# A two-layer graph network on one core: the set-up's score sums move into the feature matmul, its staging into the main pass's buffers, its stores to SyncE's queue

## The chip, the cores and the metric

The kernel runs on 1 core of one Trainium2 chip. A core has five engines, each with its own in-order instruction stream: TensorE (PE, with its weight loads listed as PEld), VectorE (DVE), ScalarE (ACT), GpSimd (POOL) and SyncE (SP). Data moves between the chip's memory (HBM) and the on-chip memory (SBUF) by DMA transfers, which SyncE, ScalarE and GpSimd issue; TensorE writes its results to a separate small memory, PSUM, of eight banks. The metric is device time in microseconds (us). The kernel before takes 2074.67 us, the median of 3 runs (2074.32 to 2076.41).

## The reference

`x` has 4096 rows of 512; `adj` is a 4096 x 4096 matrix of zeros and ones, symmetric with a full diagonal. Layer 0 is a graph attention with 8 heads of 64 features:

```python
feats = jnp.einsum('nf,hfo->hno', X, W)
s_self = jnp.einsum('hno,ho->hn', feats, a_self)
s_neigh = jnp.einsum('hno,ho->hn', feats, a_neigh)
dense = s_self[:, :, None] + s_neigh[:, None, :]
dense = jnp.where(dense > 0, dense, ALPHA * dense)
dense = dense * A[None, :, :]
attn = jax.nn.softmax(dense, axis=-1)
out = jnp.einsum('hij,hjo->hio', attn, feats) + b[:, None, :]
```

then a relu, a residual and a layer norm. Layer 1 is a dot-product attention within 32 graphs of 128 rows, with a residual and a layer norm. The change lies wholly in the preparation of layer 0: the features, the two scores of each row and head, and exponentials of the scores.

## The kernel before

**Set-up (lines 592 to 813).** `x` is taken in eight blocks `k` of four 128-row tiles `u`. For each block:

- `load_rows` (L608): SyncE loads four 128 x 512 tiles `xt_f`; the pool `xtp` has four buffers, so the next block's loads wait for this block's transposes.
- `turn_rows` (L652, L655): TensorE transposes the block, 16 pieces of 128 x 128, and ScalarE copies the four results from PSUM to `xT_f`.
- `scores` (L663, L671): TensorE multiplies the transposed block by `wa`, the 512 x 16 matrix of weights times score vectors, which VectorE makes once at the start (L638, L641); ScalarE copies the result.
- `exponentials` (L677 to L708): a small matmul with `stack` adds the four partial sums and turns them so that rows lie on partitions; ScalarE takes five exponentials for the block, VectorE splits them into parts (`e_b`, `e_p`, `nb_all`).
- `features` (L734, L742), per tile: four matmuls with 512 columns each (the four 128-row chunks of `W`, all 8 heads), then VectorE adds the bias to give `fb`.
- `scaled_features` (L748, L756, L757, L769), per tile: VectorE multiplies `fb` by an exponential (`gst`), ScalarE and VectorE make a rounded and a rest part (`fst`), and GpSimd's queue stores both to HBM (`g_d` 256 KB, `f_d` 512 KB). `fb`, `gst` and `fst` have three buffers each, in pools of the set-up's own.
- `rows_of_exponentials` and `columns_of_exponentials` (L713, L717, L721, L726, L727): the exponentials of the own score are transposed to rows, stored to `pu_d` from GpSimd's queue, and transposed back in another order.

All of these PSUM results come from one pool, `ps_setup`, of seven buffers. One more bank, `ps_misc`, is for later work. GpSimd's queue also loads the first three blocks of the adjacency with a cast to 8 bits (`load_adjacency`, L587), after blocks 3, 4 and 5.

**Main pass (`main_pass`, L1306 on).** Four passes `r`, one for each pair of heads; in each, four column blocks of 1024 and 32 tiles `j` of 128 rows, taken eight at a time in the first three passes (`wide=8`) and four at a time in the last. For each `j`, VectorE makes a tile `q` for each head from the A^T tile `at` (L1367), ScalarE a mark (L1376), and TensorE accumulates `accf` (L1387), `acc` (L1407) and `dens` (L1421). In the first pass `bring` (L1113, L1117, L1118) transposes the adjacency on TensorE, ScalarE widens it into `at`, and GpSimd's queue stores it; later passes load it back (L1103). `at` and `q` have six buffers each for the whole kernel; the first three passes have six more for `at` and two more for `q`, which `ring` hands out in turn. SyncE's queue loads `f_s`, `g_s` (the stored features, L1348, L1352), `p_row`, `u_row` (broadcast rows of `pu_d`, L1312, L1315), and `ck`, blocks of the adjacency that a check of the inputs reads. After the main pass's last steps come the pieces of layer 1, dealt into the last pass by a written plan.

**What sets the order.** TensorE's order is the program's own (`manual_schedule`); that of the other engines, and of the loads and stores on their queues, is decided when the program is built, by a scheduler that places each instruction where it expects it to be ready. On each engine, and on each queue's issuing engine, instructions then run in that fixed order. SBUF is laid out in pools; pools with `side="right"` are stacked from the other end.

Of the kernel before, what the change touches and what calls it, by code (L numbers as in the profile page):

```python
# [19 lines left out]
P = 128  # L20
# [384 lines left out]
def adjacency_streamed_path(  # L405
# [50 lines left out]
    const = ctx.enter_context(tc.tile_pool(name="fconst", bufs=1))  # L456
    first_pass = ExitStack()
# [25 lines left out]
    for c in range(FC):  # L483
# [6 lines left out]

    stack = const.tile([P, 2 * H], F32, name="stack")
    nc.vector.tensor_reduce(
        stack,
        ident.rearrange("p (c k) -> p k c", c=FC)[:, : 2 * H, :],
        AX.X,
        OP.add,
    )
# [56 lines left out]
    more = {}  # L554

    def ring(name, pool, n):

        if name not in more:
            return pool
        k = turns[name] % (n + more[name][1])  # L560
        turns[name] += 1
        return pool if k < n else more[name][0]

    def partial_sums(dst, wide, rhs):

        for c in range(FC):
            nc.tensor.matmul(
                dst[32 * c : 32 * c + 32, :], wide[:, c, :32], rhs[:, c, :], start=True, stop=True
            )
# [22 lines left out]
    with tc.tile_pool(name="setup1", bufs=1, side="right") as one, tc.tile_pool(  # L592
        name="setup2", bufs=2, side="right"
    ) as two, tc.tile_pool(name="setup3", bufs=3, side="right") as three, tc.tile_pool(
        name="xtp", bufs=4, side="right"
    ) as xtp, tc.tile_pool(name="ps_setup", bufs=7, space=PSUM) as pss:
        NB = NT // 4
        xts, xTs, sts, pu_js, rows = {}, {}, {}, {}, {}
# [13 lines left out]
        w_sb = one.tile([P, FC, H * FH], F32, name="w_sb_f")  # L612
        for c in range(FC):
            nc.scalar.dma_start(
                w_sb[:, c].rearrange("p (h o) -> p h o", h=H),
                W[:, ts(c, P), :].rearrange("h p o -> p h o"),
            )
        a_b2 = three.tile([P, PR, 2, FP], F32R, name="fst").bitcast(F32)
        a_b2 = a_b2.rearrange("p r s n -> p (r s n)").rearrange(
            "p (k h o) -> p k h o", k=2, h=H  # L620
        )
# [11 lines left out]
        wa = one.tile([P, FC, 32], F32, name="wa")  # L633
        nc.vector.memset(wa, 0.0)
        for c in range(FC):
            for k in range(2):
                prod = three.tile([P, H, FH], F32, name="fb")
                nc.vector.tensor_mul(  # L638
                    prod, w_sb[:, c].rearrange("p (h o) -> p h o", h=H), a_b2[:, k]
                )  # L640
                nc.vector.tensor_reduce(wa[:, c, k * H : (k + 1) * H], prod, AX.X, OP.add)  # L641
        xs = one.tile([P, FC, NB], F32, name="xs")

        def turn_rows(k):
# [4 lines left out]
            for u, c in order if k == 0 else sorted(order, key=lambda x: x[1]):  # L649
                if u == 0:  # L650
                    pts[c] = pss.tile([P, 4, P], F32, name="ps_set")
                nc.tensor.transpose(pts[c][:, u, :], xts[k][u][:, ts(c, P)], ident)  # L652
# [6 lines left out]
        def scores(k):  # L659

            ps = pss.tile([P, 4 * P], F32, name="ps_set")
            for c in range(FC):
                nc.tensor.matmul(  # L663
                    ps[32 * c : 32 * c + 32, :],
                    wa[:, c, :],
                    xTs[k][:, c].rearrange("p u n -> p (u n)"),
                    start=True,
                    stop=True,
                )
            st = sts[k] = one.tile([P, 4 * P], F32, name="st")  # L670
            nc.scalar.copy(st, ps)  # L671

        def exponentials(k):
            blk = slice(4 * k, 4 * k + 4)
            pts = pss.tile([P, 4, 2, H], F32, name="ps_set")
            for u in range(4):
                nc.tensor.matmul(  # L677
                    pts[:, u].rearrange("p k h -> p (k h)"),
                    tile_j(sts[k], u),
                    stack,  # L680
                    start=(u == 0),
                    stop=True,
                    skip_group_check=True,
                )
            s_c, t_c = pts[:, :, 0, :], pts[:, :, 1, :]
            nc.scalar.activation(e_all[:, blk, 1, :], t_c, AF.Exp)
            nc.scalar.activation(e_all[:, blk, 0, :], t_c, AF.Exp, scale=ALPHA)
            nc.scalar.activation(d_all[:, blk, :], t_c, AF.Exp, scale=ALPHA - 1.0)
            pu_j = pu_js[k] = two.tile([P, 4, 2, H], F32, name="pu_j")
            nc.scalar.activation(pu_j[:, :, 1, :], s_c, AF.Exp, scale=-ALPHA)  # L690
            nc.scalar.activation(pu_j[:, :, 0, :], s_c, AF.Exp, scale=1.0 - ALPHA)


# [16 lines left out]
        def rows_of_exponentials(k):  # L710
# [5 lines left out]
            row = rows[k] = one.tile([2 * H, 4 * P], F32, name="pu_row")  # L716
# [14 lines left out]
        def features(k, u):  # L731
            pf = pss.tile([P, H * FH], F32, name="ps_set")
            for c in range(FC):
                nc.tensor.matmul(  # L734
                    pf,
                    tile_j(xTs[k][:, c].rearrange("p u n -> p (u n)"), u),
                    w_sb[:, c, :],
                    start=(c == 0),
                    stop=(c == FC - 1),
                )  # L740
            fb = three.tile([P, H, FH], F32, name="fb")
            nc.vector.tensor_add(fb.rearrange("p h o -> p (h o)"), pf, b_row)  # L742
            return fb

        def scaled_features(k, u, fb):
            j = 4 * k + u
            gst = three.tile([P, PR, 2, FH], F32, name="gst")
            nc.vector.tensor_tensor(  # L748
                gst.rearrange("p r h o -> p (r h) o"),
# [4 lines left out]
            fst = three.tile([P, PR, 2, FP], F32R, name="fst")  # L754
# [10 lines left out]
            for dst, n, src in (  # L765
                (g_d, FP, gst.rearrange("p r h o -> p r (h o)")),
                (f_d, 2 * FP, fst.rearrange("p r s n -> p r (s n)").bitcast(F32)),
            ):
                nc.gpsimd.dma_start(dst[:, k, :, ts(u, n)].rearrange("r p n -> p r n"), src)  # L769

        turn_rows(0)
        for k in range(NB):
            if k + 1 < NB:
                load_rows(k + 1)
            fbs = [features(k, 0)]
            if k == 0:
                fbs.append(features(k, 1))
                scores(0)
            else:
                exponentials(k)  # L780
            if k + 1 < NB:
                turn_rows(k + 1)
            if k == 0:
                exponentials(0)
            scaled_features(k, 0, fbs[0])
            if k:
                fbs.append(features(k, 1))
                columns_of_exponentials(k - 1)
            scaled_features(k, 1, fbs[1])
            fbs.append(features(k, 2))  # L790
            scaled_features(k, 2, fbs[2])
            if k + 1 < NB:
                scores(k + 1)
            rows_of_exponentials(k)
            if k == NB - 1:
                xsum = one.tile([P, FC], F32, name="xsum")
                nc.vector.tensor_reduce(xsum, xs, AX.X, OP.add)
                xsum_b = one.tile([P, FC, 32], F32, name="xsum_b")
                nc.vector.tensor_copy(xsum_b, xsum[:, :, None].to_broadcast([P, FC, 32]))
# [729 lines left out]
```

## Time and profile before

| What | Value |
|---|---|
| Median of 3 runs | 2074.67 us (2074.32 to 2076.41) |
| Profiled execution, its own time | 2074.4 us |
| Its span, first to last instruction | 2072.1 us |
| Mean granted TensorE clock | 0.996 of full |
| Busy: TensorE / VectorE / ScalarE / GpSimd | 2040.3 / 1663.9 / 1536.7 / 247.5 us |
| Moved by DMA | 551.28 MB, mean 266 GB/s |
| First feature matmul (L734) / last one ends | 9.8 us / 161.55 us |
| First adjacency transpose (L1113) / first `accf` matmul (L1387) | 162.62 us / 168.37 us |

The page of the profile gives busy time per engine; the chain of waits follows what ended last, back through whatever released it; the windows give busy time, granted clock and DMA share in stretches of time; the groups give the number and mean time of one kind of instruction. "f32 128x512" is 128 partitions by 512 elements. Times of the windows and the chain count from the span's start.

### The profile page before, as it was taken

To read this page: it belongs to the slowest core of one execution; us is meant where nothing else is said; L and a number is where in the kernel's file an instruction comes from. 1 tells how busy PE (TensorE), PEld (TensorE's weight loads), DVE (VectorE), ACT (ScalarE), POOL (GpSimd) and SP (SyncE) were. 2 spreads that over 40 slices of the span, in tenths; PEclk is the share of its full clock that TensorE was granted. 3 is DMA by queue.
4 is the path that set the end of the run, shared out by engine and by line. 5 is a ranking of instruction groups with operands and counts; after the bars stand their busy time and mean duration, and the time that the engine had idled before them with its cause. 6 is when DMAs were issued, how large, how long until landed. Compare 5 with 4: busy or idle time off the path is not lost.

```text
span 2072.1 us, 37981 instructions
## 1 busy us (share of the span) xinstructions
PE 2040.3 (98%) x14934; PEld 999.7 (48%) x14934; DVE 1663.9 (80%) x2058; ACT 1536.7 (74%) x1821; POOL 247.5 (12%) x393
## 2 busy tenths in 40 slices
PE   8999999999999999999999999999999999999997
PEld 4555555444445444444445444544454444545443
DVE  5557888888799998798999999999975984885654
ACT  3338898888878899788889889998885666567420
POOL 2343222222100000000000000000210210210111
PEclk9999999999999999999999999999999999999999
DMA  8999999999899999788999899989974763775211
GB/s 252 265 258 248 272 293 265 296 261 297 264 332 349 361 334 338 261 312 300 315 318 337 312 342 327 325 292 361 325 234 144 245 243 132 227 272 168 71 49 43
DMA packets 207881, 551.28 MB, mean 266 GB/s; under 512 B 25292, under 2 KB 66252, under 8 KB 207692
## 3 DMA queue, kind: packets, MB, share of 16 engines
q1 hardware_dynamic: 140748, 425.79, 59.4%
q0 software_dynamic: 62784, 121.91, 23.4%
q8 instruction: 119, 1.95, 0.4%
q10 hardware_dynamic: 4160, 1.05, 0.2%
q14 instruction: 70, 0.57, 0.1%
HBM read 491.79 MB, written 107.22 MB: 289 GB/s over the span
## 4 chain that ended last, share of the span: by engine, by line
PE 81%; DMA 8%; issue 5%; DVE 3%; ACT 2%; POOL 1%; POOLq 0%; SPq 0%; DVEq 0%; ACTq 0%
PE acc L1407 35%; PE accf L1387 20%; DMA at_d<-at 5%; PE ps_m L1050 5%; PE ps_m L978 5%; PE dens L1421 5%; PE ps_set L734 4%; DVE q L1367 1%; PE ps_m L1005 1%; PE ps_m L1064 1%; ACT mark L1376 1%; DMA xt_f<-in_x_dram 1%; PE ps_m L907 1%; PE ps_m L1113 1%; PE ps_m L958 1%
## 5 line engine op out<-in xcount | busy, mean ns | idle before, releaser
L1367 DVE SCALAR_TENSOR_TENSOR q<-p_row,d_all,at 128x1024 f32<-128x1024 f32 x1024 | 1242.6, 1280 | 159.2 <-PE acc L1407 130.1
L1376 ACT ACTIVATE mark<-q,nb_all 128x1024 fp8e4<-128x1024 f32 x896 | 994.2, 1145 | 173.1 <-DVE q L1367 158.1
L1407 PE MATMUL acc<-q,g_s 128*32 128x512 f32 x8192 | 903.3, 593 | 1.1 <-DVE q L1367 0.4
L1407 PEld LDWEIGHTS acc<-q,g_s 128*32 128x32 f32 x8192 | 264.6, 110 | 594.5 <-issue 533.7
L1387 PE MATMUL accf<-at,f_s 128*128 128x512 f32 x2048 | 493.3, 397 | 1.9 <-issue 1.8
L1387 PEld LDWEIGHTS accf<-at,f_s 128*128 128x128 f32 x2048 | 379.3, 188 | 110.6 <-issue 29.1
L1132 ACT ACTIVATE ck<-ck,neg_half_f 128x1024 f32<-128x1024 f32 x128 | 146.0, 1140 | 22.1 <-DMA ck<-in_adj_dram 22.1
L1133 ACT ACTIVATE ck<-ck,neg_quarter 128x1024 f32<-128x1024 f32 x128 | 146.3, 1143 | 1.9
L1117 ACT CAST at<-ps_m 128x1024 fp32r<-128x1024 fp8e4 x128 | 120.2, 1025 | 8.7 <-PE ps_m L1113 5.6
L1421 PE MATMUL dens<-mark,e_b 128*6 128x512 fp8e4 x2048 | 124.4, 379 | 0.7 <-ACT mark L1376 0.7
L734 PE MATMUL ps_set<-w_sb_f,xT_f 128*128 128x512 f32 x256 | 117.3, 607 | 0.1
L978 PE MATMUL ps_m<-x1T,M_sb 128*128 128x512 f32 x256 | 113.1, 595 | 1.6 <-ACT x1T L959 1.6
L1050 PE MATMUL ps_m<-wvT,x1T 128*128 128x512 f32 x256 | 114.2, 594 | 0.0
L1252 POOL DMA_DIRECT2D hs_d<-hst x12 | 10.7, 894 | 834.0 <-DVE hst L1242 740.0
L1372 DVE TENSOR_SCALAR mark<-q,d_all 128x1024 fp8e4<-128x1024 f32 x128 | 96.0, 750 | 5.1 <-DVE q L1367 0.5
L1421 PEld LDWEIGHTS <-e_b 128*6 128x6 bf16 x2048 | 52.8, 86 | 80.4 <-issue 37.0
L1118 POOL DMA_DIRECT2D at_d<-at x128 | 68.8, 538 | 170.5 <-ACT at L1117 106.9
L756 ACT ACTIVATE fst<-fb 128x512 fp32r<-128x512 f32 x32 | 20.3, 636 | 83.9 <-DVE fb L742 52.9
L978 PEld LDWEIGHTS ps_m<-x1T,M_sb 128*128 128x128 f32 x256 | 47.9, 190 | 63.0 <-issue 59.9
L1050 PEld LDWEIGHTS ps_m<-wvT,x1T 128*128 128x128 f32 x256 | 47.6, 190 | 57.2 <-issue 56.0
L985 ACT ACTIVATE zT<-ps_m,zb 128x512 f32<-128x512 f32 x32 | 21.8, 683 | 71.0 <-PE ps_m L978 71.0
L734 PEld LDWEIGHTS ps_set<-w_sb_f,xT_f 128*128 128x128 f32 x256 | 49.2, 200 | 51.5 <-issue 50.2
(185 smaller groups left out, 1117.9 us busy)
## 6 DMA issues: line engine op xcount, KB each, us to landing
at<-at_d SPq DMA_DIRECT2D x384, 512.0 KB, 6.1
ck<-in_adj_dram SPq DMA_DIRECT2D x128, 512.0 KB, 5.5
f_s<-f_d SPq DMA_DIRECT2D x128, 512.0 KB, 7.3
at_d<-at POOLq DMA_DIRECT2D x128, 512.0 KB, 14.9
g_s<-g_d SPq DMA_DIRECT2D x128, 256.0 KB, 5.7
f_d<-fst POOLq DMA_DIRECT2D x32, 512.0 KB, 8.5
p_row<-pu_d SPq DMA_DIRECT2D x32, 512.0 KB, 6.9
a_b<-in_adj_dram POOLq DMA_DIRECT2D x32, 512.0 KB, 16.4
```

Of the source, the lines that this page charges most:

```text
L734: nc.tensor.matmul(pf, tile_j(xTs[k][:, c].rearrange("p u n -> p (u n)"), u), w_sb[:, c, :], start=(c == 0), stop=(c == FC - 1),)
L978: nc.tensor.matmul(pz, L1["M"][:, f, ts(c, P)], x1T[:, f, :], start=(f == 0), stop=(f == FC - 1),)
L1050: nc.tensor.matmul(pv, x1T[:, f, ts(u, P)], L1["wvT"][:, f, :], start=(f == 0), stop=(f == FC - 1),)
L1117: nc.scalar.copy(at, both[:, :, k])
L1132: tc.keep_in_program_order(nc.scalar.activation(ck, ck, AF.Square, bias=neg_half))
L1133: nc.scalar.activation(ck, ck, AF.Abs, bias=neg_quarter, accum_out=binp[:, k : k + 1])
L1367: nc.vector.scalar_tensor_tensor(q, p_row[h], d_j, ats[r, c, j].bitcast(F32), op0=OP.max, op1=OP.mult)
L1372: nc.vector.tensor_scalar(mark, q, d_j, None, op0=OP.is_gt, saturate=False)
L1376: nc.scalar.activation(mark, q, AF.Sigmoid, bias=nb_all[:, j, hh : hh + 1], scale=BIG, saturate=False,)
L1387: nc.tensor.matmul(accf[:, s, :], f_s[j // 4][:, j % 4, w, :], ats[r, c, j][:, ts(s, HB)], start=(j == 0 and w == 0), stop=(j == NT - 1 an ...
L1407: nc.tensor.matmul(acc[o : o + 32, s, :], g_s[j // 4][:, j % 4, h, o % FH : o % FH + 32], qs[j, h][:, ts(s, HB)], start=(j == 0), stop=(j ...
L1421: nc.tensor.matmul(dens[lo : lo + 6, :], e_b[:, j, 2 * r + h, :], marks[j, h][:, ts(s, HB)], start=(j == 0), stop=(j == NT - 1),)
```

## The change

- **Scores in the feature matmul.** The weight tile `w_sb` gets two more columns for each head (`FW = FH + 2`): the weights times the two score vectors. A feature matmul now gives 8 x 66 columns. Since that is more than one PSUM bank holds, it is issued as two matmuls of four heads (264 columns) each, into two banks; the features have a PSUM pool of their own, `ps_feat`, of two such pairs, and the other set-up results keep three buffers. `scores`, the `stack` matmul and `wa` go. The first three tiles are made without score columns (256 columns a matmul), and `first_scores` adds theirs with 12 small matmuls.
- **Exponentials per tile.** VectorE multiplies a tile's scores by constants (`powers`), two small instructions, and ScalarE takes three exponentials per tile instead of five per block. Their parts are made at the end of the block (`parts_of_exponentials`), and the row and column transposes of a block move into the block after it.
- **Staging.** `fb` and `gst` are the two halves of a tile of the main pass's pool `q`, `fst` is a tile of its pool `at`: six buffers each instead of three. The pool `setup3` goes.
- **Stores.** `g_d` and `f_d` are written from SyncE's queue instead of GpSimd's.
- **A^T buffers apart.** The six further `at` buffers are allocated at the start on the right side, and `ring` hands them out ahead of the first six.

```diff
@@ adjacency_streamed_path
+    wide_passes = ExitStack()
+    at2 = wide_passes.enter_context(tc.tile_pool(name="more_at", bufs=MORE, side="right"))
     first_pass = ExitStack()
...
-    stack = const.tile([P, 2 * H], F32, name="stack")
...
-    more = {}
+    more = {"at": (at2, MORE)}
 
     def ring(name, pool, n):
 
         if name not in more:
             return pool
-        k = turns[name] % (n + more[name][1])
+        pool_2, m = more[name]
+        k = turns[name] % (n + m)
         turns[name] += 1
-        return pool if k < n else more[name][0]
+        if name == "at":
+            return pool_2 if k < m else pool
+        return pool if k < n else pool_2
...
-    ) as two, tc.tile_pool(name="setup3", bufs=3, side="right") as three, tc.tile_pool(
-        name="xtp", bufs=4, side="right"
-    ) as xtp, tc.tile_pool(name="ps_setup", bufs=7, space=PSUM) as pss:
+    ) as two, tc.tile_pool(name="xtp", bufs=4, side="right") as xtp, tc.tile_pool(
+        name="setup_rows", bufs=1, side="right"
+    ) as late, tc.tile_pool(name="ps_setup", bufs=3, space=PSUM) as pss, tc.tile_pool(
+        name="ps_feat", bufs=2, space=PSUM
+    ) as psf:
...
-        w_sb = one.tile([P, FC, H * FH], F32, name="w_sb_f")
+        FW = FH + 2
+        w_sb = one.tile([P, FC, H, FW], F32, name="w_sb_f")
...
-        wa = one.tile([P, FC, 32], F32, name="wa")
-        nc.vector.memset(wa, 0.0)
         for c in range(FC):
+            prod = qp.tile([P, C], F32, name="q").rearrange("p (k h o) -> p k h o", k=2, h=H)
             for k in range(2):
-                prod = three.tile([P, H, FH], F32, name="fb")
...
-                nc.vector.tensor_reduce(wa[:, c, k * H : (k + 1) * H], prod, AX.X, OP.add)
+                nc.vector.tensor_mul(prod[:, k], w_sb[:, c, :, :FH], a_b2[:, k])
+                nc.vector.tensor_reduce(w_sb[:, c, :, FH + k], prod[:, k], AX.X, OP.add)
+        powers = one.tile([P, 5, H], F32, name="powers")
+        for i, v in enumerate((ALPHA, 1.0, ALPHA - 1.0, 1.0 - ALPHA, -ALPHA)):
+            nc.vector.memset(powers[:, i, :], v)
...
-                    pts[c] = pss.tile([P, 4, P], F32, name="ps_set")
+                    last = k == 0 and c == FC - 1
+                    pts[c] = misc([P, 4, P]) if last else pss.tile([P, 4, P], F32, name="ps_set")
...
-        def scores(k):
...
-        def exponentials(k):
+        def exponentials(k, u, sc):
+
+            j = 4 * k + u
+            if u == 0:
+                pu_js[k] = two.tile([P, 4, 2, H], F32, name="pu_j")
+            st = small.tile([P, 5, H], F32, name="st")
+            for lo, hi, w in ((0, 3, 1), (3, 5, 0)):
+                nc.vector.tensor_tensor(
+                    st[:, lo:hi].rearrange("p k (q h) -> p k q h", q=2),
+                    sc[:, None, :, :, w].to_broadcast([P, hi - lo, 2, H // 2]),
+                    powers[:, lo:hi].rearrange("p k (q h) -> p k q h", q=2),
+                    OP.mult,
+                )
+            nc.scalar.activation(e_all[:, j], st[:, 0:2], AF.Exp)
+            nc.scalar.activation(pu_js[k][:, u], st[:, 3:5], AF.Exp)
+            nc.scalar.activation(d_all[:, j, :], st[:, 2], AF.Exp)
+
+        def parts_of_exponentials(k):
...
         def features(k, u):
-            pf = pss.tile([P, H * FH], F32, name="ps_set")
+            pf = psf.tile([P, 2, HB], F32, name="ps_fe")
+            pf = pf[:, :, : H * FW // 2].rearrange("p q (h w) -> p q h w", w=FW)
+            scored = k > 0 or u == 3
+            cols = slice(0, FW if scored else FH)
             for c in range(FC):
...
+                for q in range(2):
+                    nc.tensor.matmul(
+                        pf[:, q, :, cols],
+                        tile_j(xTs[k][:, c].rearrange("p u n -> p (u n)"), u),
+                        w_sb[:, c, 4 * q : 4 * q + 4, cols],
+                        start=(c == 0),
+                        stop=(c == FC - 1),
+                    )
+            both = qp.tile([P, C], F32, name="q").rearrange("p (s h o) -> p s h o", s=2, h=H)
...
+            if scored:
+                exponentials(k, u, pf[:, :, :, FH:])
+            return both
+
+        def first_scores():
+
+            ps = pss.tile([P, 4, H, 2], F32, name="ps_set")
...
+        def scaled_features(k, u, both):
             j = 4 * k + u
-            gst = three.tile([P, PR, 2, FH], F32, name="gst")
+            fb, gst = both[:, 0], both[:, 1]
...
-            fst = three.tile([P, PR, 2, FP], F32R, name="fst")
+            fst = atp.tile([P, C], F32R, name="at").rearrange(
+                "p (r s n) -> p r s n", r=PR, s=2
+            )
...
-                nc.gpsimd.dma_start(dst[:, k, :, ts(u, n)].rearrange("r p n -> p r n"), src)
+                nc.sync.dma_start(dst[:, k, :, ts(u, n)].rearrange("r p n -> p r n"), src)
...
+            fbs = {}
+            for u in range(4):
+                fbs[u] = features(k, u)
+                if u == (0 if k else 2) and k + 1 < NB:
+                    turn_rows(k + 1)
+                if u == 1 and k:
+                    rows_of_exponentials(k - 1)
+                if u == 2 and k:
+                    columns_of_exponentials(k - 1)
+                if u == 2 and k == 0:
+                    first_scores()
+                    for v in range(3):
+                        scaled_features(k, v, fbs[v])
+                if k or u == 3:
+                    scaled_features(k, u, fbs[u])
...
+            parts_of_exponentials(k)
             if k in (3, 4, 5):
                 tc.keep_in_program_order(load_adjacency(0, 4 * (k - 3)))
+        rows_of_exponentials(NB - 1)
...
-    at2 = wide_passes.enter_context(tc.tile_pool(name="more_at", bufs=MORE))
     q2 = wide_passes.enter_context(tc.tile_pool(name="more_q", bufs=2))
-    more["at"], more["q"] = (at2, MORE), (q2, 2)
+    more["q"] = (q2, 2)
```

In the compiled order of the changed kernel, the stores stand on SyncE between the loads of `x` and the first `f_s`, `g_s`, `p_row` and `u_row` loads, and GpSimd's queue keeps, in the set-up, the `pu_d` stores and the adjacency loads.

## The prediction

> **What bounds the kernel now.** I read the page's busy times first, then its 40 slices, then the chain of waits over the set-up, then the groups by form, and last the transfers.
>
> ```profile
> span 2072.1 us, 37981 instructions
> PE 2040.3 (98%) x14934; PEld 999.7 (48%) x14934; DVE 1663.9 (80%) x2058; ACT 1536.7 (74%) x1821; POOL 247.5 (12%) x393
> ```
>
> TensorE (PE) is busy 98% of the span. The change touches the set-up alone, the first 162 us; after that TensorE's instructions stand in the same order in both kernels. TensorE never rests for long there, so what the set-up gains or loses should reach the end unchanged. One block of the set-up (four 128-row tiles) in the chain of waits:
>
> ```profile
> 93.56 1.80 PE ps_set L652 x16
> 95.35 3.44 PE ps_set L734 x8
> 98.79 0.35 PE ps_set L726 x4
> 99.14 3.64 PE ps_set L734 x8
> 102.78 1.00 PE ps_set L663 x8
> 103.78 0.54 PE ps_set L713 x4
> 104.31 6.88 PE ps_set L734 x16
> 111.19 0.84 PE ps_set L677 x8
> 112.03 1.79 PE ps_set L652 x16
> ```
>
> The reader is to see that every piece is TensorE, end to end: a block takes 112.03 - 93.56 = 18.47 us. VectorE (DVE) and ScalarE (ACT) are 50 to 60% and 30 to 45% busy there. The transfers are nearly full, though (columns: PE, PEld, DVE, ACT, POOL busy, clock, DMA share, GB/s):
>
> ```profile
> 80.00:100.00 20.00, 20.00 (x79) 10.36 (x79) 11.24 (x27) 6.70 (x20) 7.78 (x11) 1.00 0.85 247
> 100.00:120.00 20.00, 20.00 (x77) 10.31 (x76) 10.16 (x26) 6.38 (x20) 7.46 (x10) 1.00 1.06 278
> 120.00:140.00 20.00, 20.00 (x79) 9.88 (x81) 11.07 (x28) 6.14 (x19) 8.97 (x12) 1.00 1.05 215
> 160.00:180.00 20.00, 17.26 (x116) 12.85 (x118) 12.74 (x15) 16.59 (x17) 7.85 (x13) 0.83 0.87 299
> ```
>
> So the set-up is bound by TensorE, with the DMA engines close behind. The last row is the hand-over to the main pass: 2.7 us of rest and a granted clock of 0.83.
>
> **The change part by part.** *Score work on TensorE.* Per block the two score steps go: L663 1.00 us and L677 0.84 us, -1.84. In their place each feature matmul takes 264 columns twice instead of 512 once. A matmul is two passes here (256 records for 128 matmuls). L734 does 8 passes of 512 columns in 3.44 us, 0.430 each; L652 does 16 of 128 columns in 1.80, 0.1125 each. The line through both is 0.0067 us + 0.000827 us per column, so a pass of 264 takes 0.225 us and a tile's 16 passes 3.60 us: +0.16 a tile, +0.64 a block. The doubled weight loads stay hidden: with only 16 columns moving (L677) a pass with a full load takes 0.105 us, under half of 0.225. Bounds for a tile: 0.84 ns a column (0.430/512) gives 3.55, 0.88 (0.1125/128) gives 3.71; I take 3.60. Net per block -1.84 + 0.64 = -1.2, so 17.27 us.
>
> *Start.* Before, the block-1 transposes begin at 37.82 us. VectorE multiplies the weights by the score vectors until 20.05 in both kernels. After: the first feature add ends at 20.74, the third tile (256 columns, 16 x 0.218) runs to 24.3, the transposes (1.80) to 26.1, the first scores (24 passes at L677's 0.105) to 28.6, two tiles at 3.60 to 35.8. That is -2.0.
>
> *Middle.* Five blocks at -1.2: -6.0.
>
> *Last stretch.* From the seventh block's transposes to the last feature matmul the chain shows 31.1 us. Without 1.84, with seven tiles at 3.60 for 3.44 to 3.64 and one row step at 0.54 for 0.44, it is 30.4: -0.7.
>
> *Hand-over.* Before, 1.07 us lie between the last feature matmul (161.55) and the first adjacency transpose (162.62). After, the last tile's scores come out of that matmul: VectorE adds (0.69) and scales (two small operations, about 0.2 each by L727's 0.215 and L694's 0.183), ScalarE takes exponentials (0.2 each by L686), only then come the row transposes (0.54), ScalarE's copy (0.61) and the column transposes (0.35): 3.3 us, +2.2. ScalarE's last feature copy (L756, 0.63), which delayed its adjacency copies at 164.2, is earlier: -0.5.
>
> Sum: -2.0 - 6.0 - 0.7 + 2.2 - 0.5 = -7.0 us.
>
> *Waits that are new.* PSUM for features falls from a shared seven buffers to two of its own. VectorE's work per tile rises from 2.07 to about 2.5 us (three at 0.69, two at 0.2), 12.8 of 17.3 us with the 2.7 of the exponentials' parts at block end. That backlog delays the next block's first add to about 1.9 us after its matmul; its buffer is wanted 5.9 us after it, so it hides. Transposes have three buffers: the fourth group waits for ScalarE's first copy (0.6), ready about when it is wanted: 0 to 0.3 a block, taken as 0.5 in all.
>
> *The stores on SyncE's queue.* All 64 stores and the 32 loads of x now share one in-order queue with the early main-pass loads, some of which wait (f_s for its stores, p_row for pu_d, which took up to 13.0 us before). The compiled order makes every transfer wait on one of eight counters, so at most eight are under way. SyncE's issue of such a store is not in the trace: 0.39 us (L608) to 1.22 us (four W loads, 4.88 us on ScalarE), 4.7 to 11.3 us of a block: fits. The stores have six buffers (26 us of cover) instead of three, so their landing hides. The x loads are what counts. The next block but one's loads stand behind the store of tile 0, about 5 us after its matmul, and are wanted a block later: 12.2 us of slack.
>
> ```profile
> L608 SPq DMA_DIRECT2D xt_f<-in_x_dram x32: 327/390/1303, 0.7 to 115.0; - x32
> DMA to landing us min/median/max: 3.0/6.4/15.9
> ...
> f_d<-fst POOLq DMA_DIRECT2D x11, 512.0 KB, 10.6
> xt_f<-in_x_dram SPq DMA_DIRECT2D x4, 256.0 KB, 7.1
> ```
>
> The first pair is the whole set-up, the last two lines are 100 to 150 us. Landing like the stores, 10.6, the loads are in time by 1.6 us; at 15.9 each of five turns loses 3.7, 18.5 in all. A gain is excluded, since after 20 us TensorE's only wait in the set-up is 0.8 us for L671's copy. I take 1.0 in all, nearer to 10.6.
>
> [...]
>
> *Clock.* In the hand-over it fell to 0.50 though the longest rest was 1.83 us:
>
> ```profile
> 164.00:165.00 1.00, 0.00 (x0) 0.00 (x0) 0.17 (x2) 1.00 (x3) 0.61 (x2) 0.74 0.26 82
> 165.00:166.00 1.00, 0.23 (x3) 0.23 (x3) 0.90 (x2) 1.00 (x2) 0.29 (x2) 0.50 0.80 250
> ```
>
> That cost 1.3 us (L1387's first 32 passes 8.72 us, the next 7.38). It stays. The start gets a rest of its own (18.6 to 20.8 us): 0 to +1.3. I take 0, since 20 to 25 us, as sparse, kept 1.00 before.
>
> [...]
>
> *Free by cover:* the five small memsets (VectorE waits for the score vectors until 9.2), 96 small exponentials for 40 (ScalarE stays under half busy), and the A^T buffers apart: the first six A^T tiles of pass 0 were free before too. The first Q tiles wait for the last stores; the sixth is wanted about 10 us after the last feature matmul and they land at about that time; without that cover, 1 to 2 us.
>
> With +0.5 and +1.0 the change is -5.5 us. Against the profiled execution, 2074.4 us (span 2072.1 and 2.3 around it, 0.3 under the median 2074.67), that is **2068.9, so 2069.0 us**.
>
> **The rivals.** *A, x loads eat half of it:* two or three turns late by 1 to 2 us while the casting adjacency loads fill the DMA (share 1.06). For it: f_d waits already cost ScalarE 23.1 us. Against: the longer cover. Price +3 to +5: 2071 to 2074.
> *B, slower:* one mechanism, x loads late at every turn, because SyncE stands behind waiting loads and stores. For it: the 15.9 us seen once; against: medians of 6.4 and 7.1. At 15.9 us: 2074.4 - 6.5 + 18.5 = 2086. It decides from a mean landing of 12.2 + 6.5/5 = 13.5 us.
> *C, it does not do what it says:* the halves cost what the score steps did. A tile must reach 3.44 + 0.46 = 3.90 us, a pass 0.244; then a block saves nothing, two tiles of the start and seven of the last stretch cost 0.3 more each, and the sum is -1.4 + 0 + 1.4 + 2.2 - 0.5 + 1.5 = +3.2: 2077.6. Against it: both rows of pass lengths.
> *D, more:* no x wait, the hand-over hidden in the earlier ScalarE work: -8 to -9, 2065.5 to 2066.5.
>
> **How the numbers follow.** 0.2% (4.1 us) is about what a measurement of this kernel can tell from no change. The forecast (2066.5 to 2070.5) has 0.52, A 0.20, B 0.12, C 0.06, D 0.10. Faster: forecast and D, 0.62. Same: A, C and the nearest of B, 0.28. Slower: the rest of B, 0.10. The range leaves out the far end of B and the edge of D: 2065.0 to 2077.0.
>
> **What would show it.** Right: the feature line at 3.6 us a tile; blocks of about 17.3 us in the chain; the last feature matmul ending at 153 to 154.5 us instead of 161.55; a hand-over of 3 us; the first accf matmul at about 163 instead of 168.4; the main pass as long as before. A: short "DMA xt_f" pieces from the fourth block on. B: such pieces in every block, and SyncE waiting for its own counters. C: L719's passes at 0.24 us. The prediction falls if the main pass changes length, if VectorE appears in the set-up's chain beyond the ends, or if the clock falls at 20 us.

## The result, and the profile after

The changed kernel takes 2083.07 us, the median of 6 runs (2082.19 to 2087.17); the kernel before took 2074.49 us beside it (2072.58 to 2077.89). The ratio is 1.0042, with a 95% interval of 1.0031 to 1.0052: 0.42% longer, and above the forecast's range. The profiled execution took 2082.19 us.

```profile
span 2080.3 us, 38361 instructions
PE 2038.3 (98%) x15086; PEld 1046.7 (50%) x15086; DVE 1667.6 (80%) x2125; ACT 1540.4 (74%) x1869; POOL 190.7 (9%) x329
```

The span is 8.2 us longer, while TensorE's busy time is 2.0 us shorter: it does a little less work and stands still more. An undisturbed block in the chain of waits looks as forecast:

```profile
35.82 1.94 PE ps_set L649 x16
37.76 3.57 PE ps_fe L719 x16
41.33 0.44 PE ps_set L694 x4
41.76 3.57 PE ps_fe L719 x16
45.33 0.35 PE ps_set L707 x4
45.68 7.33 PE ps_fe L719 x32
53.01 1.93 PE ps_set L649 x16
```

A feature tile takes 3.57 us, the score steps are gone, and the block takes 53.01 - 35.82 = 17.19 us where it took 18.47. But from 68 us on the chain leaves TensorE:

```profile
67.96 8.69 DMA p_row<-pu_d
...
76.71 12.46 DMA xt_f<-in_x_dram
89.17 11.71 DMA f_d<-at
...
100.94 11.28 DMA xt_f<-in_x_dram
...
112.27 3.03 PE ps_set L649 x13
```

A p_row load, an x load, a store and another x load follow one another; SyncE's queue held the first of these x loads 0.4 us for the p_row load and the second 3.2 us for the store. TensorE's waits from 20 to 165 us, and the same windows as before (PE, PEld, DVE, ACT, POOL busy, clock, DMA share, GB/s):

```profile
PE ps_set L649 <- DMA xt_f<-in_x_dram: 7.1, 3, 4.7
```

```profile
80.00:100.00 20.00, 18.12 (x92) 15.46 (x93) 11.13 (x36) 6.96 (x26) 1.43 (x2) 1.00 1.12 276
100.00:120.00 20.00, 14.79 (x70) 12.87 (x69) 8.09 (x26) 5.51 (x22) 0.00 (x0) 0.91 1.09 257
...
160.00:180.00 20.00, 16.64 (x103) 13.65 (x105) 14.30 (x28) 16.49 (x20) 6.72 (x11) 0.74 0.90 200
```

Around the end of the longest wait (4.7 us, to 112.27) the granted clock is 0.50, from 111.9 to 115.3 us: 13 transposes take 3.03 us where 16 take 1.87. So the first `accf` matmul starts at 169.6 us, 1.2 us later than before, instead of some 5 us earlier.

The main pass is longer too, though the change lies in the set-up. I took the starts of the 80 `accf` stages from both traces (0 to 47 in passes 0 to 2, 48 to 79 in pass 3). From 1.2 us the delay creeps to 4.1 us at the start of pass 3; 1.7 us of that lie within stages 1 to 47 themselves, about 0.04 us each. During the first column block of pass 3 the delay doubles to 8.2 us, after a peak of 9.8; after that it stays. The chain at that place, where before there was TensorE alone:

```profile
1372.31 0.37 SPq L1149
...
1372.79 5.96 DMA hp_l<-hs_d
...
1378.88 0.09 DVE x1b L1156
...
1379.35 2.49 DVE q L1375 x2
```

On VectorE an addition of `hp_l` (rows needed only for layer 1) stands ahead of the Q tiles: it began at 1378.88 us and they at 1379.35. Its load was issued late, at 1372.79. So there are three questions: the x loads, the creeping, and pass 3.

### The profile page after: what moved, and what is told of

Read it like the earlier page. It is cut to its first block, busy times and chain, and to the rows that moved or that the text cites. A ratio compares the mean times of both kernels' runs of the same rounds, so it can differ in the third digit from the quotient of the medians.

```text
span 2080.3 us, 38361 instructions
## 1 busy us (share of the span) xinstructions
PE 2038.3 (98%) x15086; PEld 1046.7 (50%) x15086; DVE 1667.6 (80%) x2125; ACT 1540.4 (74%) x1869; POOL 190.7 (9%) x329
## 3 DMA queue, kind: packets, MB, share of 16 engines
q8 instruction: 120, 1.97, 0.4%
q10 hardware_dynamic: 4160, 1.05, 0.2%
## 4 chain that ended last, share of the span: by engine, by line
PE 78%; DMA 10%; issue 6%; DVE 4%; ACT 2%; POOL 1%; SPq 0%; POOLq 0%; DVEq 0%; ACTq 0%
PE acc L1415 34%; PE accf L1395 19%; DMA at_d<-at 5%; PE ps_m L1058 5%; PE ps_m L986 5%; PE dens L1429 4%; PE ps_fe L719 4%; DVE q L1375 2%; PE ps_m L1013 1%; PE ps_m L1072 1%; DMA xt_f<-in_x_dram 1%; DMA a_b<-in_adj_dram 1%; DMA hp_l<-hs_d 1%; PE ps_m L915 1%; PE ps_m L1121 1%
## 5 line engine op out<-in xcount | busy, mean ns | idle before, releaser
L719 PE MATMUL ps_fe<-w_sb_f,xT_f 128*128 128x264 f32 (+1 forms) x512 | 120.3, 392 | 1.8 <-DVE q L727 1.6
L719 PEld LDWEIGHTS ps_fe<-w_sb_f,xT_f 128*128 128x128 f32 x512 | 99.9, 199 | 16.2 <-DVE q L727 2.0
L1066 DVE TENSOR_TENSOR v_t<-ps_m,bv_row 128x512 f32<-128x512 f32 x32 | 21.9, 686 | 61.8 <-PE ps_m L1058 61.8
```

Source lines behind the costliest of these rows:

```text
L719: nc.tensor.matmul(pf[:, q, :, cols], tile_j(xTs[k][:, c].rearrange("p u n -> p (u n)"), u), w_sb[:, c, 4 * q : 4 * q + 4, cols], start=(c ...
```

## The experiments

Times come from different chips, so each ratio is against the kernel before on the same chip. "First accf" is the start of the first `accf` matmul (168.4 us before, 169.6 changed); "x waits" is TensorE's waiting for x between 20 and 165 us. These two come from one profiled execution of each kernel, which can lie off the median: it took 2083.29 us in e7 and 2080.09 us in e1.

| Run | Median us | Ratio (95%) | x waits us | First accf us |
|---|---|---|---|---|
| changed | 2083.07 | 1.0042 (1.0031 to 1.0052) | 7.1 | 169.6 |
| e1 | 2077.58 | 1.0002 (0.9993 to 1.0012) | 3.0 | 165.1 |
| e2 | 2083.19 | 1.0033 (1.0020 to 1.0046) | 8.2 | 173.5 |
| e3 | 2078.23 | 1.0015 (1.0004 to 1.0027) | 0 | 167.0 |
| e4 | 2073.11 | 0.9987 (0.9978 to 0.9996) | 2.7 | 165.2 |
| e5 | 2073.88 | 0.9983 (0.9974 to 0.9992) | 2.6 | 166.5 |
| e6 | 2071.13 | 0.9970 (0.9959 to 0.9982) | 0 | 160.0 |
| e7 | 2076.63 | 0.9998 (0.9988 to 1.0007) | 0 | 170.2 |
| e8 | 2074.70 | 0.9988 (0.9979 to 0.9997) | 0 | 169.0 |
| e9 | 2068.92 | 0.9964 (0.9951 to 0.9977) | 0 | 160.1 |
| e10 | 2083.90 | 1.0032 (1.0019 to 1.0045) | 4.3 | 168.4 |
| e11 | 2077.79 | 1.0004 (0.9995 to 1.0012) | 0.7 | 169.4 |
| e12 | 2067.29 | 0.9958 (0.9946 to 0.9970) | 0 | 159.7 |

**e1: the stores back on GpSimd's queue.**

```diff
-                nc.sync.dma_start(dst[:, k, :, ts(u, n)].rearrange("r p n -> p r n"), src)
+                nc.gpsimd.dma_start(dst[:, k, :, ts(u, n)].rearrange("r p n -> p r n"), src)
```

> Theory: the set-up lost its gain because the stores of g_d and f_d went to SyncE's queue, ahead of the x loads. With the stores back on GpSimd's queue and all else as changed, TensorE's waits of 7.1 us for x at L649 are gone, the last feature matmul ends at about 154 us instead of 160.5, and the first accf matmul starts at about 163.3 instead of 169.9; the stall at the start of pass 3 (4.1 us) and the slow drift of passes 0 to 2 (2.8 us) stay. Time about 6.5 us under the changed kernel's 2083.1: 2076.5. Rival: the staging in six A^T and six Q buffers, or VectorE's backlog, is what delays the set-up; then the x waits and the first accf matmul at 169 to 170 stay, and the time is 2082 to 2084.

The first accf came 4.5 us earlier and the time fell to the kernel before's. The theory holds for most of it, the staging rival falls. But the waits did not vanish: 3.0 us stayed, and the clock was 0.91 from 120 to 140 us. Something else also makes a load late. In pass 3 the delay still jumped, by 3.1 us at the second stage, of which 2.0 us were left at stage 60.

**e2: the old order of the A^T buffers.**

```diff
-        if name == "at":
-            return pool_2 if k < m else pool
```

> Here only the order in which the twelve A^T buffers are handed out is put back (the six of the old pool first, then the six apart). Theory: the stall at the start of pass 3 comes from that order, because the twelve-buffer rounds of passes 0 to 2 now end on the six buffers that pass 3 goes on with, so its A^T loads and, behind them on SyncE, the hp_l loads come late. The accf groups 48 to 60 then no longer gain 4.1 us on the kernel before. The first A^T tiles of pass 0 wait for the last staged f_d stores instead, 0 to 2 us. Time 2083.1 - 4.1 + 0 to 2: 2079 to 2081. Rival: the stall comes from the place of the six buffers or from the later start of everything; then it stays, and the time is 2082 to 2085.

The jump is gone from the trace: between stages 48 and 60 the delay grows by 0.9 us, not 4.1. The other profiles divide the same way: it grows by 2.0 to 2.3 us in e1, e3 and e10, which have the new order, and by 0.9 us at most in those with the old one. So the order costs some 2 us; why it was 4.1 in the changed kernel's profile stays open. VectorE's instructions in the main pass stand again as in the kernel before. VectorE's longest waits between 1365 and 1470 us, changed kernel and then e2 (4.9 us in the kernel before):

```profile
DVE x1b L1156 <- DMA hp_l<-hs_d: 8.2, 4, 3.6
```

```profile
DVE x1b L1154 <- DMA hp_l<-hs_d: 5.6, 4, 2.9
```

The time hardly moved, however (1.0033 against 1.0042, with overlapping intervals): this execution reached the main pass 3.9 us later. Of that, 1.7 us is a fall of the clock at 29 to 33 us and 1.1 us longer x waits, neither of which the edit touches; 1.1 us is unexplained. The expected 2079 to 2081 was a miss, but the place of the stall was right. Why the order matters is read from the code: passes 0 to 2 use 384 A^T tiles, 32 full rounds of twelve. In the new order a round ends on the six old buffers, the only ones pass 3 has, so its A^T loads have to wait for them, and the scheduler puts the `hp_l` loads and their additions elsewhere.

**e3: only the x loads on GpSimd's queue.**

```diff
-                nc.sync.dma_start(xt, x[ts(4 * k + u, P), :])
+                nc.gpsimd.dma_start(xt, x[ts(4 * k + u, P), :])
```

> The changed kernel with the x loads alone moved to GpSimd's queue; the stores stay on SyncE's, one packet for each row. Theory Q (the loads stand behind stores that wait in SyncE's queue): the waits for x at L649 fall from 7.1 us to under 1.5 us, the first accf matmul starts at 163 to 165 us, time 2076 to 2078.5. Theory P (the stores' many packets, 42,428 on the hardware queue in the first 235 us against 8,745 before, fill the DMA engines whatever queue the loads are on): at least 4 us of waits for x stay, first accf matmul at 168 to 170, time 2081 to 2084.

No wait for x is left, with the stores as they were. The transfers of e3 from 20 to 160 us:

```profile
DMA packets 38861, 36.58 MB, mean 261 GB/s; under 512 B 1677, under 2 KB 36046, under 8 KB 38848
```

The 62 stores in that time have 31,744 rows of 0.5 or 1 KB. From SyncE's queue they travel as about one packet for each row: 36,046 packets are under 2 KB, where the kernel before has 4,752, and there are 2.6 times as many packets in all (14,875 before, for 36.05 MB). Yet the loads are on time: theory P falls, Q stands. The start was worse than expected, since the first x loads on GpSimd's queue left the weight load late (TensorE waits 1.8 us for it at 18.5 us); the clock also falls to 0.50 at 33 us, where the first scores end (see e12).

**e4: stores on GpSimd's queue, old order, staging in the buffers apart** (e1 and e2, and this):

```diff
-        a_b2 = atp.tile([P, C], F32R, name="at").bitcast(F32)
+        a_b2 = at2.tile([P, C], F32R, name="at").bitcast(F32)
...
-            fst = atp.tile([P, C], F32R, name="at").rearrange(
+            fst = at2.tile([P, C], F32R, name="at").rearrange(
```

> The changed kernel with the stores on GpSimd's queue, the old order of the A^T buffers, and the staging of the features in the six A^T buffers apart instead of the six of the old pool. Theory: with both causes gone, what is left is the work taken off TensorE: first accf matmul at 162.5 to 164 us (168.6 in the kernel before), main pass as long as before, 2067.5 to 2070.5, 4 to 7 us under the kernel before. Rival: the set-up's gain is lost on the way through the main pass, or the staging costs it; then 2072 to 2079.

This beats the kernel before, by 0.13%, but not by the 0.2% or more expected. Pass 3 is nearly right (+0.9 us); the x waits of 2.7 us remain, and so does the creeping (3.2 us from the first stage to pass 3).

**e5: the addresses.**

```diff
     nc.vector.tensor_copy(ident_b, ident)
+    room = const.tile([P, 16], F32, name="room")
+    nc.vector.memset(room, 0.0)
...
+    ) as late, tc.tile_pool(name="setup_st", bufs=3, side="right") as stp, tc.tile_pool(
...
-            st = small.tile([P, 5, H], F32, name="st")
+            st = stp.tile([P, 5, H], F32, name="st")
```

> e4 with nothing moved in any queue: the small st tiles go to a pool of their own on the right side and a 64-byte constant is added, so that all buffers on the left side (A^T, Q, f_s, g_s, marks, rows) have the addresses of the kernel before again, 416 bytes lower than in the changed kernel; the six A^T buffers apart and the two more Q buffers stay where the change put them. Theory: the slow drift is the addresses. 22 accf stages between 640 and 1180 us take 165.0 us in the kernel before and 165.9 to 166.0 in all changed ones (7.494 against 7.545 us each), 48 of them 2.4 us; with the old addresses they take 165.0 again and the time is 2073.1 - 2.4 = 2070.7. Rival: the place of the six A^T buffers apart does it; then the stages stay at 7.545 us and the time at 2073.

The `accf` group between 640 and 1180 us, in e4 and in e5 (last column: mean ns):

```profile
L1393 PE MATMUL accf<-at,f_s 128*128 128x512 f32 x711 | 170.4, 397 | 0.0
```

```profile
L1395 PE MATMUL accf<-at,f_s 128*128 128x512 f32 x715 | 170.3, 395 | 0.0
```

The 22 stages there (18 to 39) take 165.02 us, to a hundredth the kernel before's, against 166.03 in e4; 22 `acc` stages take 302.64 in all three. On every engine and queue the instructions of e4 and e5 stand in the same order, but for the one memset. So the creeping is the buffers' addresses, and nothing in the queues. In e4 the extra time repeats every three stages, about 0.10, 0.01 and 0.04 us, and three stages of eight A^T tiles are two rounds of the ring of twelve; this points at the A^T buffers. In the changed kernel, which hands them out in another order, the pattern is another, and the 22 stages take 165.92. The time itself doesn't prove the 2.4 us: the ratio fell by 0.0004, inside the intervals, and this execution lost 1.7 us at the start.

```profile
20.15 5.41 PE L719 MATMUL ps_fe<-w_sb_f,xT_f 128*128 128x256 f32 x16 [2.05 <-DVE q L727]
```

The third tile takes 5.41 us, 3.73 in the changed kernel's profile: after a rest of 2.05 us the granted clock is 0.50 from 22 to 25 us.

**e6: e4 with the first p_row loads behind the last x loads.**

```diff
-                nc.sync.dma_start(p_row[h], broadcast_rows(pu_d[2 * r + h, ts(c, C)], P, C))
+                d = nc.sync.dma_start(p_row[h], broadcast_rows(pu_d[2 * r + h, ts(c, C)], P, C))
+                if r == 0 and c == 0:
+                    tc.keep_in_program_order(d)
```

> e4 with the first p_row loads of pass 0 (four of 512 KB) held behind the last x loads in SyncE's queue. Theory: what is left of the x waits in e4 (2.7 us in three waits at 123 to 126 us, one x load of 15.4 us in the chain, then a granted clock of 0.91 for 20 us) comes from the p_row pair that is issued at 104.97 us, ahead of the last four x loads. Without it the waits fall under 0.5 us, the clock stays at 1.00 and the first accf matmul starts at 161.5 to 162.5 us instead of 165.4: time 2073.1 - 3.4 = 2069.7. Rival: the stores and the casting adjacency loads on GpSimd's queue make the load late; then 2 to 3 us of waits stay and the time is 2073.

SyncE's queue in e4, at the last x loads:

```profile
104.97 1.29 SPq L1318 DMA_DIRECT2D p_row<-pu_d  x2
106.79 3.78 SPq L605 DMA_DIRECT2D xt_f<-in_x_dram  x4
```

With the pair out of the way, no wait for x is left and the chain from 104.61 to 121.73 us is TensorE alone. The first accf starts at 160.0 us, 8.4 us before the kernel before's, where the prediction had summed 7.0 for the removed work. The time (2071.1) is 1.4 us over the expected 2069.7; the profiled execution took 2067.6.

**e7: e4 with the stores on SyncE's queue and, from the second block, the x loads on GpSimd's** (e3's edit with `nc.gpsimd if k else nc.sync`).

> e4's staging and order of the A^T buffers, but the stores on SyncE's queue as in the changed kernel, and the x loads on GpSimd's queue from the second block on (the first block's stay on SyncE's). Theory: loads and stores on different queues are enough, whichever is on which; no waits for x, the start as in the changed kernel (second block's turn at 35.9 us) and not as in e3, which started 2 to 3 us later; the first accf matmul at 163 to 164.5 us, time 2070 to 2072.5. Rival: the stores' small packets on the hardware queue cost the set-up more; first accf matmul at 166 to 168, time 2074 to 2076.

A miss, in the median too (2076.6 us); the profile caught the slowest of twelve executions. No x waits, but the weight load was late again (a rest of 3.40 us before 17.66 us, clock 0.50 from 17 to 24), so the first block's place in the queue was not what had cost e3 its start. From 125 to 140 us TensorE also stood still for 2.9 us: ScalarE waited 10.3 us for f_d stores to land (two waits, between 100 and 150 us), so even six buffers did not cover them there.

**e8: the kernel before with its stores on SyncE's queue,** and nothing else.

> The kernel before with one part of the change alone: its stores of g_d and f_d on SyncE's queue. Theory: the x loads stand behind stores that wait for their data and for SyncE's counters, and TensorE waits for x here too, 3 to 7 us, a little less than the 7.1 us in the changed kernel as a block takes 18.5 us instead of 17.2 and gives more cover; time 2078 to 2082. Rival: the 18.5 us hide it, only the faster blocks of the change bring the loads on the path; waits under 1 us, 2074.5 to 2076.

The rival is right: no wait for x, and the time is, if anything, lower (0.9988). The move of the stores alone is harmless when a block takes 18.5 us, but only just: in two turns the last x load landed about 1 us before TensorE began the turn (111.5 against 112.5 us, 130.1 against 131.0). That the length of the block decides is argued, since the changed kernel differs in its staging and its other loads too.

**e9: e5 and e6 together.**

> e5 and e6 together: stores on GpSimd's queue, staging in the A^T buffers apart, old order of the A^T buffers, first p_row loads behind the last x loads, and the left-side buffers at the addresses of the kernel before. Theory: the two gains add, as one lies in the set-up (first accf matmul at 160.2 us in e6, 168.6 in the kernel before) and one in TensorE's own pace in passes 0 to 2 (2.4 us): 2071.1 - 2.4 = 2068.7, 0.33 to 0.45% under the kernel before. Rival: the shorter accf stages are taken back by waits of VectorE or by loads in the main pass; then 2070.5 to 2071.5.

2068.9, as expected, 0.36% under the kernel before. That the two gains add is less sure: e6 and e9 have overlapping intervals, and in e9's profile 1.6 us was lost at one place in pass 0, whose cause I have not tested.

**e10: the changed kernel with e6's edit alone.**

> The changed kernel with one thing different: the first four p_row loads of pass 0 held behind the last x loads in SyncE's queue, where the stores stay. Theory: the stores alone were hidden in e8 and the p_row loads cost e4 3 to 5 us, so the changed kernel's 7.1 us of waits for x are the work of both; without p_row 2 to 4 us of waits stay, first accf matmul at 165 to 167.5 us instead of 169.9, time 2079 to 2081. Rival: in the faster blocks the stores are enough by themselves; then at least 6 us of waits stay and the time is 2082 to 2084.

Between the two. The waits fell from 7.1 to 4.3 us, by 2.8, where e1 without the stores lost 4.1 of them; so p_row is part of it and the stores are more. But the time did not fall. This execution lost 1.7 us to the clock at the start and 4.2 us at one place in pass 0 (the tenth `accf` stage), where TensorE waits 2.6 us for ScalarE's marks and the clock falls (0.58 from 408 to 412 us). e1 lost 3.7 us at the same place, the changed kernel's profile 0.5, the runs with the old order at most 0.3. That was not tested.

**e11: the kernel before, its left-side buffers 352 bytes higher.**

```diff
+    room = const.tile([P, 88], F32, name="room")
+    nc.vector.memset(room, 0.0)
     stack = const.tile([P, 2 * H], F32, name="stack")
```

> The kernel before with a constant of 352 bytes added, so that its left-side buffers (A^T, f_s, Q and the rest) lie 352 bytes higher and, as in the changed kernel, at multiples of 64 bytes; nothing else. Theory: TensorE's accf stage slows with that address, to about 7.54 us from 7.494 in the kernel before, 48 stages in passes 0 to 2, so the time is 2.0 to 2.5 us longer: 2077 to 2078.5 where the kernel before is at 2075.5 on the same chip. Rival: another property of the address counts (a distance between two buffers, or a multiple larger than 64), and 352 bytes leave the stage at 7.49 and the time unchanged.

The 22 stages take 165.06 us: unchanged. Lying at multiples of 64 bytes is not enough. Here all twelve A^T buffers moved together; in the changed kernels six of them moved by 416 bytes and the other six lie on the right side, so a distance between them remains possible. Which property counts stays open.

**e12: e9 with the rest at the start filled.** The twelve transposes write a tile that nothing reads.

```diff
             for u in range(4):
+                if k == 0 and u == 2:
+                    pt = pss.tile([P, 4, P], F32, name="ps_set")
+                    for i in range(12):
+                        nc.tensor.transpose(pt[:, i % 4, :], ident, ident)
                 fbs[u] = features(k, u)
```

> e9 with twelve transposes of the identity into an unused PSUM tile between the second and the third feature tile of the first block, where TensorE waits for VectorE's first feature add (rests of 1.36 to 2.15 us in the runs so far). Theory: in the runs whose rest was 2.05 us or more the granted clock fell to 0.50 between 22 and 34 us and 32 passes took 9.06 us instead of 7.37; with most of the rest filled no execution pays this 1.7 us, which about half paid: the rest at 18 to 20 us falls under 1 us, the clock stays at 1.00 to 40 us, time 0.3 to 1.2 us under e9: 2067.7 to 2068.6. Rival: the clock falls for another reason or the executions that paid were few; then the time is e9's 2068.9 within 0.3 us, or up to 0.5 more if the added work delays the third tile.

```profile
18.52 1.47 PE L790 MATMUL ps_set<-ident_f 128*128 128x128 f32 x12
20.00 3.73 PE L719 MATMUL ps_fe<-w_sb_f,xT_f 128*128 128x256 f32 x16
```

No rest, clock 1.00 throughout 16 to 36 us, and 2067.3 us, the fastest: 0.42% under the kernel before. Against e9 the intervals overlap, so the filling itself is shown in the trace, not in the time.

The theory that the rest makes the clock fall fits e5, but not e2 and e10. In the record of the granted clock the falls begin on a grid with steps of 3.41 us: two of the changed kernel's profile, at 111.9 and 163.1 us, lie 51.20 us or 15 steps apart, two of e7's, at 16.9 and 34.0 us, five. The grid lies differently in each execution: e5's fall begins at 21.60 us and e2's at 29.28, 2.25 steps later. In e5 the step before the fall held 1.97 us of the rest. In e2 and e10 the rest lies across two steps, about 1.05 us in each, and two more steps pass before the fall. The second of these was filled for 2.76 and 2.77 us by the first scores, 24 passes of only 16 columns (e2, then the changed kernel):

```profile
25.63 3.00 PE L739 MATMUL ps_set<-w_sb_f,xT_f 128*128 128x16 f32 x24
28.48 9.06 PE L717 MATMUL ps_fe<-w_sb_f,xT_f 128*128 128x264 f32 x32
```

```profile
25.60 3.00 PE L741 MATMUL ps_set<-w_sb_f,xT_f 128*128 128x16 f32 x24
28.45 7.37 PE L719 MATMUL ps_fe<-w_sb_f,xT_f 128*128 128x264 f32 x32
```

The same 3.00 us fall into two steps in the changed kernel's profile (0.95 and 2.05 us), and the next 32 passes run at full clock. The falls of e3 at 33 us and of e7 at 34 us follow the first scores too (2.84 and 2.91 us in one step). The twelve transposes fill the rest and leave the first scores as they are. In e12's profile those lay across two steps (1.77 and 1.23 us), which was luck and not the filling.

## Why the prediction was wrong

- *TensorE's pieces* were right: 3.57 us a tile for 3.60, a block of 17.19 for 17.27, the turn of the second block at 35.82 for 35.8. Rival C, for which a tile had to reach 3.90 us, falls with that. The hand-over was +2.5 us for +2.2 (the feature matmuls end at 160.43, the adjacency transposes start at 164.03; before, 1.07). In e6, with the loads out of the way, the gain at the first accf is 8.4 us for the 7.0 summed, which is rival D's size.
- *The stores on SyncE's queue*, for which 1.0 us of waits was taken, is the step that failed in the set-up: the waits were 7.1 us. It weighed how long an x load takes to land against 12.2 us of slack, and took the load to leave about 5 us after its buffer came free:

```profile
L607 SPq DMA_DIRECT2D xt_f<-in_x_dram x32: 327/432/2405, 0.7 to 120.8; - x32
DMA to landing us min/median/max: 3.2/5.9/12.7
```

  In the median the loads landed faster than the 10.6 us assumed, but the two that held TensorE up longest took 12.46 and 11.28 us. The first left 4.7 us after its buffer came free, about as assumed, and was late by its landing, by 1.9 us. At the second turn 5.2 us were lost, mostly to the issue: the load that TensorE missed for 4.7 us left at 100.94 us, 9.7 us after the transposes that freed its buffer, having waited 3.2 us for the counter of an f_d store, behind stores that were waiting for VectorE. SyncE's DMA instructions between 20 and 140 us, summed from the trace, last 73.8 us, 14.8 before. That is 10.6 us a block, inside the 4.7 to 11.3 that "fits" took: the total fits, and a load waits for its place all the same (single stores took up to 4.75 us).
- Rival B named this mechanism and gave it 0.12, but as a landing time at every turn. It came at two turns and cost 7.1 us of waits and about 1.5 us of slower transposes (3.03 us for 13, at 1.87 for 16). Its condition, a mean landing of 13.5 us, was not met: what it left out is the time in the queue.
- Rival A's late loads are real too (3.0 us in e1, with the stores gone; one load took 15.4 us to land in e4), but e6 shows that p_row broadcasts ahead in the queue make them, not the casting adjacency loads.
- *The A^T buffers apart, costed at nothing* looked only at pass 0. The price was at the other end of the ring: 4.1 us in pass 3 (0.9 in e2), of which some 2 us recur in every profile with the new order.
- *"The main pass as long as before"* is the other step that failed. It fell on that, and on the addresses, which no list of instructions shows: 1.7 us in stages 1 to 47 of the changed kernel (2.5 in e4 and e6, with the old order). The first stage is 0.4 us longer, and 0.8 us between the stages of passes 0 to 2 are not explained.
- *The clock at the start*, 0 to +1.3 and taken as 0: in the changed kernel's profile it was 0; in e2, e5 and e10 it was 1.7. The prediction had only the rest in mind, which e5 paid for; e2 and e10 paid after the first scores, work that the change itself puts there.

The forecast had the first accf 5.5 us earlier and the main pass unchanged; of the 13.7 us that the profile lies above that, 6.7 arose in the set-up and 7.0 after it. The 8.2 us of span are 1.2 in the set-up (a gain of 8.4 that late loads, with the clock, turned into a loss), 2.9 in passes 0 to 2 and 4.1 in pass 3. Two of the three parts lie outside the functions that I thought to be the whole of the change.

## What to carry to other kernels

Before moving transfers to another queue, write down that queue's whole order and ask when each transfer can be issued, not only how fast it lands; the same stores that were free in e8 (18.5-us blocks) were the larger part of 7.1 us of waits in the changed kernel (17.2-us blocks). A ring of buffers has to be followed to its last round, since the order that is free at the start decides which buffers the next phase finds in use. Compare the main loop's stages at equal positions in both traces: a few hundredths of a microsecond a stage, and a stall far from the edit, show there at once and nowhere in the diff.

## What the runs showed of the hardware

- TensorE's `accf` stage took 7.50 or 7.55 us in the mean of 22 (165.02 or 166.03 us) depending on the addresses of the buffers alone (e5 against e4, 416 bytes apart on the left side); 352 bytes made no difference (165.06 us in e11).
- The falls of the granted clock to 0.50, but for the last in a trace, lasted 6.83 us in the kernel before, 3.41 and 10.24 us in the changed kernel's profile, and at the start 3.4 us in e2, e3, e5 and e10 and 6.8 and 3.4 us in e7: one, two or three steps of 3.41 us. At the start (14 to 40 us) a fall followed a step with 1.97 or 2.62 us of rest (e5, e7) and a step with 2.76 to 2.91 us of 16-column matmuls (e2, e3, e7, e10). None followed the 1.50 us of rest in e9 or the step with 2.05 us of such matmuls in the changed kernel's profile.
- From 20 to 160 us the 62 stores have 31,744 rows of 0.5 or 1 KB. With them on SyncE's queue the changed kernel has 35,613 packets under 2 KB, about one for each row; with them on GpSimd's queue the kernel before has 4,752 (39,961 packets against 14,875 in all, for 36.2 and 36.1 MB). No load came late for it in e3 or e8 (38,861 and 40,037 packets).
